# A two-layer graph kernel on one core: eight places lent once, the first 128 chunks of `src` and x loaded first, the rest of `src` and `dst` turned later

## The chip, the core and the metric

The kernel runs on one core of one Trainium2 chip. The metric is the device time of one execution in microseconds. The core has five instruction streams that matter here: TensorE (PE) for matrix products, VectorE (DVE), ScalarE (ACT), GpSimd (POOL), which issues the indirect DMAs (gathers of rows by a list of indices), and SyncE (SP), which issues the plain DMAs. Each stream runs in its written order and waits on semaphores for the others.

## The reference

x has 6250 rows of 512 floats; `src` and `dst` are the two ends of 100,000 edges, sorted by `dst`.

```python
h = jnp.maximum(_layernorm(x, axis=-1), 0.0)
norm = -dinv[src] * dinv[dst]                 # dinv = 1/sqrt(number of edges that leave a node), or 0
def _cheb_conv(x, src, dst, norm, W0, W1, b):
    out = x @ W0
    tx1 = segment_sum(x[src] * norm[:, None], dst, num_segments=N)
    return out + tx1 @ W1 + b
h = _cheb_conv(h, src, dst, norm, W1_0, W1_1, b1)
h = _layer_norm(h, gamma, beta)
h = jnp.where(h >= 0, h, 0.01 * h)
out = _cheb_conv(h, src, dst, norm, W2_0, W2_1, b2)
return x + out
```

## The kernel before

**Chunks and steps.** The sorted edges are cut into NC = 782 chunks of 128. For each layer, one gather on GpSimd fetches the 128 source rows of a chunk (256 KB) into a *place* in SBUF. A 128x32 matrix `sel` of zeros and ones then adds them up by target node: `ps[32 rows] += sel.T @ rows`. Three chunks make a unit with its own 32 rows of `ps`, four units make a step, so a step sums 12 chunks (L630, in `sums`), in the order s = 0, 1, 2 and within it q = 0 to 3. There are NS = 66 steps (`g` in `usual_path`); step 0 has one unit and chunks 0 to 2, step g has chunks 12g - 9 to 12g + 2, and the last step has 11. The sums of a step are copied to `agg` (L641), and `place` (L661) distributes them over blocks of 128 nodes with a second matrix, `there`. For each of the 49 node blocks there are then the transposes (L526 for the block's own rows `h`, L769 for the summed rows `an`) and the products with the two weight matrices (L538), a layer norm in layer one, and the stores.

**Places.** A gather needs a free place. There are X = 12 lent ones at first (the two weight tiles `w`, 4 places each, and the four bias tiles, which are loaded with their own contents later) and those of the tile `places`, with 63 rows of 528 floats. The last 8 of its rows are kept for the second layer's weights (`w_late`), so R = 55 are left, and chunk k uses row `(k - X) % R`. Chunk k can be gathered once chunk k - 55 has been summed. The first RAW = 76 chunks are gathered from x itself, before the table of normalised rows is complete, and are normalised in their place afterwards (`find`, `look_up`, L483 to L509). Later chunks come from the table `tab`, whose 16 extra columns carry `dinv`.

**The setup** (up to about 108 us). SP loads `src_i`, the chunk form of `src` and `dst`, and x, block by block, into rows 14 to 62 of `places`. `src` has to be turned, so that a chunk lies along the partitions: cast by VectorE, transposed by TensorE (L233), copied to `sidx` by ScalarE (L235); only then can GpSimd issue its first gather (L239). `dst` is turned likewise into `dlx` (L257 to L261). VectorE counts the edges of each source node: 25 groups, in each of which two comparisons make matrices `lo` and `hi` (L343) that TensorE multiplies (L357). ScalarE meanwhile computes means and variances of the x blocks (`stats`) and normalises them (`make_table`, L314); SP writes a pair of blocks to `tab`, and the two places of that pair can then take a gather (`gather_raw`). `turns` says at which counting group which x blocks are taken.

**The order of the work.** In the setup, only SP's order is the written one and the other engines' is set by a scheduler from the dependences; `issue_after` keeps an instruction behind another. In the main part, TensorE, GpSimd and SP follow the program's order (`manual_schedule`). There, a step first issues the gathers that are allowed (`gather_to`), then works off the blocks that are complete (`finished`, which calls `turn` with the transposes of `h` and `place`), then makes `sel` and takes its sums. In the steps of `SOON` = 4 and 5 of layer one, the sums come ahead of `finished`.

**The end of a layer.** In step 64 and 65 the sums are cut into pieces with the work of the last blocks between them; `place_end` (L684), `end_block` (L692) and `end_products` treat the last block, with 106 rows.

Of the kernel before, what the change touches and what calls it, by code (L numbers as in the profile page):

```python
# [20 lines left out]
P = 128  # L21
# [22 lines left out]
def gnn_kernel(  # L44
# [111 lines left out]
    for lo, hi in parts(EP):  # L156
        nc.sync.dma_start(src_i[lo:hi], src[lo * EJ : hi * EJ].rearrange("(p j) -> p j", j=EJ))


    nc.gpsimd.memset(eps, EPS)  # L160
    nc.gpsimd.memset(places[:, :, D:], 1.0)
    nc.scalar.activation(root_eps, eps, AF.Sqrt)
    FG = NC // P - (E % (P * P) == 0)
    chunks = []
    for ids, fill, name in ((src, 0, "src_c"), (dst, NO_NODE, "dst_c")):
        t = ep.tile([P, NG, P], I32, name=name)
        nc.gpsimd.memset(t[:, FG:, :], fill)
        nc.sync.dma_start(t[:, :FG, :], ids[: FG * P * P].rearrange("(g c e) -> c g e", c=P, e=P))
# [7 lines left out]
        chunks.append(t)  # L176


# [15 lines left out]
    nc.gpsimd.memset(places[:, RE + NB - 1, :D], 0.0)  # L194
    for i0, n in groups[:6]:
        load_x(i0, n)

    def load_rest(k):
# [6 lines left out]
        if k == 4:  # L205
            for t, v in ((bias1, b1), (bias2, b2), (gam, gamma), (bet, beta)):
# [7 lines left out]
    nc.gpsimd.iota(diff, pattern=[[1, P]], base=0, channel_multiplier=-1,  # L214
                   allow_small_or_imprecise_dtypes=True)
# [6 lines left out]
    nc.gpsimd.memset(ones, 1.0)  # L222


    nc.vector.tensor_single_scalar(ident, diff, 0.0, op=OP.is_equal)
    with tc.tile_pool(name="turn", bufs=1) as wp, tc.tile_pool(
        name="turn_ps", bufs=2, space=bass.MemoryType.PSUM
    ) as wps:
        f = wp.tile([P, NG, P], F32, name="f")
        nc.vector.tensor_copy(f, chunks[0])  # L230
        for g in range(NG):
            fT = wps.tile([P, P], F32, name="fT")
            nc.tensor.transpose(fT, f[:, g, :], ident)  # L233
            n = min(P, NC - g * P)
            nc.scalar.activation(sidx[:, g * P : g * P + n], fT[:, :n], AF.Copy)  # L235

    def gather_raw(lo, hi):
        for t in range(lo, min(hi, X + R)):
# [5 lines left out]

    low = ep.tile([P, P], I32, name="low")
    nc.vector.tensor_single_scalar(low, chunks[0][:, 0, :], P - 1, op=OP.bitwise_and)
    nc.vector.tensor_copy(src_lo, low)
    nc.vector.tensor_copy(pick, ident)


    nc.vector.memset(dlx[:, 0:1], 0.0)
    nc.vector.memset(dlx[:, 1 + NC :], float(N))
    with tc.tile_pool(name="turn", bufs=1) as wp, tc.tile_pool(
        name="turn_ps", bufs=1, space=bass.MemoryType.PSUM
    ) as wps:
        f = wp.tile([P, NG, P], F32, name="f")
        nc.vector.tensor_scalar_add(f, chunks[1], 1.0)  # L257
        dl_ps = wps.tile([P, NG * P], F32, name="dl_ps")
        for g in range(NG):
            nc.tensor.transpose(dl_ps[:, g * P : (g + 1) * P], f[:, g, :], ident)  # L260
        nc.scalar.activation(dlx[:, 1 : 1 + NC], dl_ps[:, :NC], AF.Copy)  # L261
        last = ident[:, P - 1 : P]
        first_ps = nodes_ps[:, : NQ * NS + 1]
        nc.tensor.matmul(first_ps, last.to_broadcast([P, P]), dlx[:, 0 : STEP * NQ * NS + 1 : STEP], start=True, stop=True)
        nc.vector.tensor_copy(first, first_ps)
        row_ps = wps.tile([P, NS], F32, name="row_ps")
        for q in range(NQ):
            for g, n in ((0, 1), (1, NS - 1)):
# [54 lines left out]
    for k in range(2):  # L323
        stats(*some[k])

    both = ep.tile([P, NB, 2, 2], F32, name="both")
    with tc.tile_pool(name="deg", bufs=1) as dp, tc.tile_pool(name="onehot", bufs=2) as ohp, tc.tile_pool(
# [11 lines left out]
        for g in range(EJ // (2 * GJ)):  # L339
# [9 lines left out]
            if k is not None:  # L349
# [4 lines left out]
                if k + 2 < len(some):  # L354
                    stats(*some[k + 2])
# [53 lines left out]
def usual_path(tc, have):  # L409
# [19 lines left out]
    with ExitStack() as es:  # L429
# [175 lines left out]
        def scale(sel, chunk, of=(0, NQ)):  # L605
# [4 lines left out]
            if end <= RAW:  # L610
                return
# [704 lines left out]
```

## Time and profile before

| | us |
|---|---|
| median of 3 runs | 2026.56 (2023.77 to 2027.43) |
| profiled execution | 2031.79 |
| span in that profile | 2030.0 |
| TensorE busy | 1662.7 (82%) |
| GpSimd busy | 1522.9 (75%) |
| VectorE busy | 708.7 (35%) |
| ScalarE busy | 414.0 (20%) |
| first gather issued at | 8.14 |
| last gather issued at | 2009.57 |

The profile is of one execution. A line of a timeline gives start, duration, engine, source line, operation, output and input, the number of instructions merged, and in brackets the idle time of the engine ahead of it with what ended that. A line of groups gives busy time and mean duration, then the idle time ahead and what ended most of it; "issue" there means that the engine waited for nothing that the profile shows. For a row by stage the columns are the stretch, its length, busy time by engine with the number of instructions, the granted TensorE clock, the share of time that the DMA engines were busy, and GB/s. A DMA instruction on GpSimd is busy while it is issued; its data land later.

### The profile page before, as it was taken

How to read it: one execution, taken by the hardware profiler on the slowest of the kernel's cores; microseconds unless marked ns; L12 is line 12 of the kernel's file. 1: busy time of each engine (PE TensorE's matmuls, PEld its weight loads, DVE VectorE, ACT ScalarE, POOL GpSimd, SP SyncE). 2: the span in 40 equal slices, each digit the busy share in tenths (PEclk: the TensorE clock that was granted, in tenths of full speed). 3: DMA queues.
4: the chain of work that ended last, by engine and by line, in shares of the span. 5: the costliest groups of instructions: out<-in, count | busy, mean ns of one | idle time of the engine just before them, and what ended most of it. 6: DMA issues, size and time to landing. Idle time of an engine off the chain costs nothing.

```text
span 2030.0 us, 20088 instructions
## 1 busy us (share of the span) xinstructions
PE 1662.7 (82%) x6907; PEld 667.6 (33%) x6907; DVE 708.7 (35%) x1494; ACT 414.0 (20%) x750; POOL 1522.9 (75%) x1578
## 2 busy tenths in 40 slices
PE   4579998777887776878879888888888888888987
PEld 3544443223333222333323322323322332333333
DVE  7965543332453333443453111122211212222211
ACT  8795221111221111221211100101010101011100
POOL 7867777777777777777777777777777777777774
PEclk9779998889898889989998998999998999999999
DMA  9998888888888888888887888888887888788875
GB/s 343 374 355 247 268 277 254 253 244 261 282 276 261 248 254 250 267 254 267 242 259 239 257 251 251 243 255 248 245 257 246 245 253 256 240 262 252 272 236 165
DMA packets 190115, 528.40 MB, mean 260 GB/s; under 512 B 34637, under 2 KB 36411, under 8 KB 190005
## 3 DMA queue, kind: packets, MB, share of 16 engines
q0 software_dynamic: 125120, 415.88, 68.4%
q1 hardware_dynamic: 64844, 111.14, 15.2%
q8 instruction: 56, 0.92, 0.2%
q14 instruction: 55, 0.44, 0.1%
q10 hardware_dynamic: 40, 0.02, 0.0%
HBM read 475.25 MB, written 51.66 MB: 260 GB/s over the span
## 4 chain that ended last, share of the span: by engine, by line
PE 45%; DMA 25%; POOL 12%; issue 10%; DVE 6%; ACT 1%; POOLq 0%; DVEq 0%; SPq 0%; ACTq 0%
DMA places<-tab,sidx 19%; PE u_ps L538 18%; PE ps L630 14%; POOL places L450 12%; PE an_ps L661 8%; DMA places<-tab,lidx 5%; PE hT_ps L526 2%; PE hT_ps L769 2%; DVE hi L343 1%; DVE lo L343 1%; PE hT_ps L498 1%; DMA h<-tab 1%; DVE sel L617 0%; DVE st L729 0%; DMA tab<-places 0%
## 5 line engine op out<-in xcount | busy, mean ns | idle before, releaser
L450 POOL DMA_INDIRECT places<-tab,sidx x1191 | 1130.6, 949 | 368.0 <-issue 262.6
L630 PE MATMUL ps<-places,sel 128*32 128x512 f32 x3104 | 505.1, 660 | 149.9 <-DMA places<-tab,sidx 84.9
L661 PE MATMUL an_ps<-agg,there 128*128 128x512 f32 (+1 forms) x554 | 273.7, 627 | 96.2 <-ACT agg L641 90.9
L450 POOL DMA_INDIRECT places<-tab,lidx x270 | 255.4, 946 | 82.2 <-issue 62.4
L630 PEld LDWEIGHTS ps<-places,sel 128*32 128x32 f32 x3104 | 100.7, 116 | 520.6 <-issue 182.8
L577 DVE TENSOR_TENSOR sel<-dlx,nodes_ps 128x384 f32<-128x384 f32 (+3 forms) x134 | 72.3, 541 | 409.8 <-PE ps L630 409.8
L538 PE MATMUL u_ps<-w,hT 128*128 128x512 f32 (+1 forms) x400 | 184.9, 606 | 21.2 <-ACT hT L528 20.5
L641 ACT ACTIVATE agg<-ps 128x512 f32<-128x512 f32 (+1 forms) x128 | 76.0, 593 | 565.2 <-PE ps L630 539.2
L538 PE MATMUL u_ps<-places,hT 128*128 128x512 f32 (+2 forms) x408 | 183.2, 593 | 3.2 <-ACT hT L528 3.2
L661 PEld LDWEIGHTS an_ps<-agg,there 128*128 128x128 f32 (+1 forms) x554 | 106.6, 201 | 219.6 <-issue 110.7
L538 PE MATMUL u_ps<-w,aT 128*128 128x512 f32 x384 | 173.4, 594 | 2.6 <-DVE aT L771 2.5
L538 PE MATMUL u_ps<-places,aT 128*128 128x512 f32 x384 | 173.4, 593 | 0.8 <-DVE aT L771 0.8
L617 DVE TENSOR_TENSOR sel<-sel,places 128x384 f32<-128x384 f32 (+11 forms) x71 | 34.3, 488 | 339.2 <-DMA places<-tab,sidx 328.6
L720 DVE TENSOR_TENSOR u_ps<-u_ps,bias 128x512 f32<-128x512 f32 x45 | 31.5, 700 | 282.5 <-PE u_ps L538 282.5
L528 ACT ACTIVATE hT<-hT_ps 128x512 f32<-128x512 f32 (+1 forms) x98 | 58.2, 594 | 279.7 <-PE hT_ps L526 278.9
L649 DVE TENSOR_SCALAR there<-iota_r,node_of 128x128 f32<-128x128 f32 (+1 forms) x286 | 86.2, 304 | 70.6 <-PE an_ps L661 68.0
L762 ACT ACTIVATE an<-an_ps,ndinv 128x512 f32<-128x512 f32 x96 | 65.8, 685 | 216.4 <-PE an_ps L661 216.4
L538 PEld LDWEIGHTS u_ps<-w,hT 128*128 128x128 f32 (+1 forms) x400 | 73.5, 194 | 97.0 <-issue 74.7
L732 ACT ACTIVATE sd<-mv,eps 128x1 f32<-128x1 f32 (+1 forms) x49 | 14.4, 294 | 437.8 <-DVE mv L730 431.1
L538 PEld LDWEIGHTS u_ps<-places,hT 128*128 128x128 f32 (+1 forms) x408 | 74.7, 193 | 77.5 <-issue 72.1
L538 PEld LDWEIGHTS u_ps<-w,aT 128*128 128x128 f32 x384 | 70.4, 190 | 83.4 <-issue 76.9
L538 PEld LDWEIGHTS u_ps<-places,aT 128*128 128x128 f32 x384 | 70.6, 190 | 80.3 <-issue 78.3
(193 smaller groups left out, 1341.1 us busy)
## 6 DMA issues: line engine op xcount, KB each, us to landing
places<-tab,sidx POOLq DMA_INDIRECT x1191, 4.0
h_tab<-g SPq DMA_DIRECT2D x48, 256.0 KB
xt<-in_x_dram SPq DMA_DIRECT2D x48, 256.0 KB
out_dram<-t SPq DMA_DIRECT2D x48, 256.0 KB
tab<-t SPq DMA_DIRECT2D x46, 256.0 KB
tab<-places SPq DMA_DIRECT2D x22, 528.0 KB
h<-tab SPq DMA_DIRECT2D x45, 256.0 KB
h<-h_tab SPq DMA_DIRECT2D x45, 256.0 KB
```

What stands on the lines that cost most here:

```text
L343: nc.vector.tensor_tensor(t, s[:, g * 2 * GJ : (g + 1) * 2 * GJ].rearrange("p (j s) -> p j s", s=2)[:, :, None, :] .to_broadcast([EP, GJ, ...
L450: nc.gpsimd.indirect_dma_start(out=places[:, (t - X) % R, :] if own_scale else zr(layer, t), out_offset=None, in_=x if layer == 0 and t < ...
L526: nc.tensor.transpose(ps[:, kc, :r], h[:r, kc * P : (kc + 1) * P], ident[:r, :r])
L528: nc.scalar.activation(hT[:, :, :r], ps[:, :, :r], AF.Copy)
L538: nc.tensor.matmul(u_ps[:r], hT[:, kc, :r], w[:, kc, :], start=(start and kc == 0), stop=(stop and kc == KD - 1))
L577: nc.vector.tensor_tensor(sel[:, q : q + k, :w, :], of, node[:, q : q + k, None, :].to_broadcast([P, k, w, Q]), op=OP.is_equal)
L630: nc.tensor.matmul(ps[q * Q : (q + 1) * Q, :], sel[:, q, s, :], zr(layer, chunk[q][s]), start=(s == 0), stop=(s == len(chunk[q]) - 1 and ( ...
L641: nc.scalar.activation(agg[g][: n * Q], ps[: n * Q], AF.Copy)
L649: behind[1] = nc.vector.tensor_scalar(t[:m, :r], iota_r[:m, :r], node_of[:m, g : g + 1], -(1.0 + i * P), op0=OP.subtract, op1=OP.is_equal)
L661: nc.tensor.matmul(placed[i][:r], t[:m, :r], agg[g][:m, :], start=(g == inside[i][0]), stop=(g == inside[i][-1]))
L762: nc.scalar.activation(an[:r], placed.pop(i)[:r], AF.Copy, scale=ndinv[:r, i : i + 1])
L769: nc.tensor.transpose(ps[:, kc, :r], an[:r, kc * P : (kc + 1) * P], ident[:r, :r])
```

## The change

Five things are changed.

1. *The order of loading.* SP issues the first 128 chunks of `src` (one 128x128 piece) first, then the first x blocks, and the rest of `src`, `dst` and `src_i` between further x blocks. Two fills of `places` on GpSimd go behind its iotas; `ident` is made first.
2. *Turning in pieces.* Only the first 128x128 piece is cast, transposed and copied to `sidx` ahead of the first gather. The other pieces of `src` are turned in counting group 1 and `dst` in group 2, each cast in its own tile.
3. *Eight places lent.* The last eight rows of `places` are used once, for chunks 67 to 74 (`gather_raw` goes up to `X + RE + NB` = 75); `slot` gives the row of a chunk, and in layer one `gather_to` allows eight chunks more up to chunk 129. From chunk 130 on it is again 55 chunks.
4. *`SOON`* is 3 to 5 instead of 4 and 5.
5. *The ends.* In layer two, step 64 takes its sums for the first two units of the step, then for the other two. The last `agg` copy and the copy of `end_block` are cut into halves.

The program order of SP at the start, before:

```order
1 L157 DMA src_i<-in_src_dram 112x800
2 L157 DMA src_i<-in_src_dram 13x800
3 L168 DMA src_c<-in_src_dram 128x6x128
4 L171 DMA src_c<-in_src_dram 13x128
5 L174 DMA src_c<-in_src_dram 1x32
6 L168 DMA dst_c<-in_dst_dram 128x6x128
7 L171 DMA dst_c<-in_dst_dram 13x128
8 L174 DMA dst_c<-in_dst_dram 1x32
9 L188 DMA places<-in_x_dram 128x2x512
10 L188 DMA places<-in_x_dram 128x4x512 x3
11 L188 DMA places<-in_x_dram 128x7x512 x2
```

And the same place on SP now:

```order
1 L160 DMA src_c<-in_src_dram 128x128
2 L186 DMA places<-in_x_dram 128x2x512
3 L196 DMA src_i<-in_src_dram 112x800
4 L196 DMA src_i<-in_src_dram 13x800
5 L186 DMA places<-in_x_dram 128x4x512
6 L160 DMA src_c<-in_src_dram 128x5x128
7 L165 DMA src_c<-in_src_dram 13x128
8 L168 DMA src_c<-in_src_dram 1x32
9 L186 DMA places<-in_x_dram 128x4x512
10 L160 DMA dst_c<-in_dst_dram 128x6x128
11 L165 DMA dst_c<-in_dst_dram 13x128
12 L168 DMA dst_c<-in_dst_dram 1x32
```

One 128x128 piece of `src` and two x blocks have moved to the front; `dst` has moved behind ten x blocks.

TensorE at step 3 of layer one, before:

```order
949 L483 MATMUL hT_ps<-src_lo,pick 128x128
950 L526 MATMUL hT_ps<-ident,h 128x128 x4
951 L661 MATMUL an_ps<-agg,there 128x512
952 L661 MATMUL an_ps<-pre,there 128x512
953 L661 MATMUL an_ps<-agg,there 128x512
954 L630 MATMUL ps<-places,sel 32x512 x12
955 L498 MATMUL hT_ps<-sc,xt 128x98 x4
```

And now:

```order
954 L510 MATMUL hT_ps<-src_lo,pick 128x128
955 L657 MATMUL ps<-places,sel 32x512 x12
956 L553 MATMUL hT_ps<-ident,h 128x128 x4
957 L690 MATMUL an_ps<-agg,there 128x512
958 L690 MATMUL an_ps<-pre,there 128x512
959 L690 MATMUL an_ps<-agg,there 128x512
960 L525 MATMUL hT_ps<-sc,xt 128x98 x4
```

The twelve sums of step 3 stand ahead of the transposes of `h` and of the first placement.

TensorE in the last steps of layer two, before:

```order
1793 L661 MATMUL an_ps<-agg,there 128x512 x3
1794 L630 MATMUL ps<-places,sel 32x512 x4
1795 L769 MATMUL hT_ps<-ident,an 128x128 x4
1796 L630 MATMUL ps<-places,sel 32x512 x4
1797 L538 MATMUL u_ps<-places,aT 128x512 x4
1798 L630 MATMUL ps<-places,sel 32x512 x4
1799 L661 MATMUL an_ps<-agg,there 128x512 x2
1800 L630 MATMUL ps<-places,sel 32x512 x5
```

And now:

```order
1798 L690 MATMUL an_ps<-agg,there 128x512 x3
1799 L657 MATMUL ps<-places,sel 32x512 x4
1800 L800 MATMUL hT_ps<-ident,an 128x128 x4
1801 L657 MATMUL ps<-places,sel 32x512 x2
1802 L565 MATMUL u_ps<-places,aT 128x512 x4
1803 L657 MATMUL ps<-places,sel 32x512 x6
1804 L690 MATMUL an_ps<-agg,there 128x512 x2
1805 L657 MATMUL ps<-places,sel 32x512 x5
```

The twelve sums of step 64 are cut into 4, 2 and 6 instead of 4, 4 and 4, and the first six are those of two units.

The diff, cut to its core:

```diff
+    load_chunks(chunks[0], src, 0, 1)
+    nc.gpsimd.iota(diff, pattern=[[1, P]], base=0, channel_multiplier=-1,
+                   allow_small_or_imprecise_dtypes=True)
+    made = nc.vector.tensor_single_scalar(ident, diff, 0.0, op=OP.is_equal)
...
+    load_x(*groups[0])
+    for lo, hi in parts(EP):
+        nc.sync.dma_start(src_i[lo:hi], src[lo * EJ : hi * EJ].rearrange("(p j) -> p j", j=EJ))
+    load_x(*groups[1])
+    load_chunks(chunks[0], src, 1, FG)
+    load_end(chunks[0], src)
+    load_x(*groups[2])
+    load_chunks(chunks[1], dst, 0, FG)
+    load_end(chunks[1], dst)
+    for i0, n in groups[3:6]:
         load_x(i0, n)
...
+    def turn_src(wps, to, lo, hi):
+        copied = nc.vector.tensor_copy(to, chunks[0][:, lo:hi])
+        for g in range(lo, hi):
+            fT = wps.tile([P, P], F32, name="fT")
+            nc.tensor.transpose(fT, to[:, g - lo, :], ident)
+            n = min(P, NC - g * P)
+            turned = nc.scalar.activation(sidx[:, g * P : g * P + n], fT[:, :n], AF.Copy)
+        return copied, turned
...
     def gather_raw(lo, hi):
-        for t in range(lo, min(hi, X + R)):
+        for t in range(lo, min(hi, X + RE + NB)):
...
+            if g in (1, 2):
+                with tc.tile_pool(name="turn_ps", bufs=3 - g, space=bass.MemoryType.PSUM) as wps:
+                    (turn_rest, turn_dst)[g - 1](wps)
...
-    SOON = range(4, 6)
+    SOON = range(3, 6)
...
+        LATER = places.shape[1] - R
+        def slot(k):
+            return k - X if k < X + R + LATER else (k - X - LATER) % R
...
+            end = summed_to + R
+            if layer == 0:
+                end = max(end, min(end + LATER, X + LATER + 2 * R))
...
+                w = D // 2 if g == NS - 1 else D
+                for lo in range(0, D, w):
+                    nc.scalar.activation(agg[g][: n * Q, lo : lo + w], ps[: n * Q, lo : lo + w], AF.Copy)
...
+            for lo in range(0, KD, KD // 2):
+                nc.vector.tensor_copy(aT[:, lo : lo + KD // 2, :r], ps[:, lo : lo + KD // 2, :r])
...
-                    step = [[(s, q) for q in range(NQ)] for s in range(STEP)]
+                    if layer:
+                        half = [[(s, q) for s in range(STEP) for q in range(at, at + NQ // 2)] for at in (0, NQ // 2)]
+                        step = [half[0][:-2], half[0][-2:], half[1]]
+                    else:
+                        step = [[(s, q) for q in range(NQ)] for s in range(STEP)]
```

More of the change, by code (lines that the diff above doesn't have):

```diff
@@ L322, in gnn_kernel @@
     turns = {1: 0, 4: 1, 7: 2, 11: 3, 17: 4, 21: 5}
-    for k in range(2):
-        stats(*some[k])
+    with tc.issue_after(turned.ins):
+        for k in range(2):
+            stats(*some[k])
     both = ep.tile([P, NB, 2, 2], F32, name="both")
```

141 lines of the change are left out of this document (66 added, 75 removed).

## The prediction, before the result was known

> **What bounds the kernel now.** I read the page first, then GpSimd's groups and its busy time by stage, then its timeline at every place where it idled longer than usual, then TensorE and the end. In the page, POOL is not the busiest engine; the row of its groups says why it still bounds.
>
> ```profile
> PE 1662.7 (82%) x6907; PEld 667.6 (33%) x6907; DVE 708.7 (35%) x1494; ACT 414.0 (20%) x750; POOL 1522.9 (75%) x1578
> ...
> L450 POOL DMA_INDIRECT places<-tab,sidx x1191 | 1130.6, 949 | 368.0 <-issue 262.6 <-DMA places<-tab,sidx 52.4 <-PE ps L630 26.5
> ...
> 0.00:8.14 8.14, 3.66 (x14) 1.00 0.75 212
> 8.14:92.19 84.05, 71.86 (x41) 0.90 1.02 375
> 92.19:128.60 36.41, 27.57 (x30) 0.72 1.03 366
> 128.60:152.02 23.42, 12.44 (x13) 0.78 1.05 331
> 152.02:2010.52 1858.50, 1407.34 (x1482) 0.93 0.83 254
> 2010.52:2030.00 19.48, 0.00 (x1) 0.97 0.18 60
> ```
>
> The columns of the last six rows are: stretch, its length, POOL's busy time and instructions, granted TensorE clock, DMA share, GB/s. From 152.02 to 2010.52 there are 1482 gathers in 1858.50 us, one per 1.254 us (0.949 busy and 0.30 of issue), with nothing else between them. GpSimd issues without a pause for 92% of the span, so the end is: when GpSimd leaves 152, plus a fixed number of gathers, plus the 19.48 us behind the last one. Only four things can be shortened: the 8.14 us ahead of the first gather, the slow stretch to 92.19, the hole before 152.02, and the tail.
>
> The slow stretch: 40 gathers (the 41st begins at its border) in 84.05 us, where 40 x 1.254 = 50.2 would do, so 33.9 us are lost. The timelines of VectorE and GpSimd say to whom.
>
> ```profile
> 28.71 1.78 DVE L343 TENSOR_TENSOR hi<-s_hi,iota_g 125x3136 bf16<-125x3136 bf16 x1
> 30.41 1.22 DVE L343 TENSOR_TENSOR lo<-s_lo,iota_g 125x2048 bf16<-125x2048 bf16 x1
> 31.55 1.78 DVE L343 TENSOR_TENSOR hi<-s_hi,iota_g 125x3136 bf16<-125x3136 bf16 x1
> ...
> 28.78 2.53 POOL L239 DMA_INDIRECT places<-in_x_dram,sidx  x1 [0.30 <-issue]
> 31.62 2.53 POOL L239 DMA_INDIRECT places<-in_x_dram,sidx  x1 [0.30 <-issue]
> ...
> 92.19 0.95 POOL L239 DMA_INDIRECT places<-in_x_dram,sidx  x1 [0.30 <-issue]
> ```
>
> A gather that begins 0.07 us behind a `hi` takes 2.53 us instead of 0.95, and ends about 0.9 us after that `hi` does; then the next one begins just behind the next `hi`. GpSimd falls into step with the 2.84 us of a counting group and issues one gather per group. The last `hi` is over before 92.19, and from there each takes 0.95, though the DMA share stays 1.03. So I put the loss down to VectorE's 25 counting groups, not to the DMA engines: 33.9 / 25 = 1.36 us a group, 1.59 (2.84 - 1.25) where it is locked. [...]
>
> **The change, part by part.** *Earlier first gather.* The chain of before:
>
> ```profile
> 0.74 0.89 SPq L157 DMA_DIRECT2D src_i<-in_src_dram  x2
> 2.68 0.25 SPq L174 DMA_DIRECT2D src_c<-in_src_dram  x1
> ...
> 5.85 0.23 DVE L246 TENSOR_SCALAR low<-src_c 128x128 int32<-128x128 int32 x1 [4.94 <-DMA src_c<-in_src_dram]
> 6.25 0.62 DVE L230 CAST f<-src_c 128x896 f32<-128x896 int32 x1
> 7.07 0.69 PE L233 MATMUL fT<-ident,f 128*128 128x128 f32 x2 [7.07 <-DVE p_i L274]
> 7.58 0.49 ACT L235 ACTIVATE sidx<-fT 128x128 int32<-128x128 f32 x2 [5.34 <-PE fT L233]
> 8.14 1.10 POOL L239 DMA_INDIRECT w<-in_x_dram,sidx  x1 [3.91 <-ACT sidx L235]
> ```
>
> Now the 128x128 piece of `src` is SP's first DMA instead of its third to fifth; SP issued its first at 0.74. From the end of the last issue to VectorE's read were 5.85 - 2.93 = 2.92 us; 0.74 + 0.40 + 2.92 = 4.06 is the late end for the new landing, and 3.0 the early one (a smaller DMA, nothing ahead of it). Behind it: a 128x128 copy as `low`, 0.23; transpose 7.07 to 7.58, 0.51; ScalarE to GpSimd 0.56; 1.3 together. The first gather is issued between 4.3 and 5.4; GpSimd's own start-up (3.66 us busy from 0.74 on, the same instructions reordered) ends at 4.2 either way. I take 4.9, a gain of 3.2 (2.7 to 3.8). It is kept only if the counting costs the same 33.9 us, and it is the same 25 groups; locked in all of them it would be 39.8, which is 5.9 worse, and I allow as much the other way.
>
> *Counting earlier, rest turned later.* `src_i` keeps its place near the front (third), VectorE no longer does the seven-column casts and `dst` first, and the first x block no longer stands behind eight other DMAs, so ScalarE starts its sums some 4 us before the 10.68 of before:
>
> ```profile
> 10.68 0.63 ACT L294 ACTIVATE junk<-places 128x512 bf16<-128x512 f32 x1 [1.98 <-DMA places<-in_x_dram]
> ...
> 16.54:91.07 74.53, 45.29 (x399) 39.70 (x399) 73.66 (x68) 65.24 (x154) 64.47 (x34) 0.89 1.02 375
> ```
>
> In this row (PE, PEld, DVE, ACT, POOL busy) VectorE is full from 16.54 to 91.07 and ScalarE 88%, so both follow an earlier start. Against it: the turned pieces now sit inside groups 1 to 5, where TensorE's counting matmuls queue behind transposes of `dst`, and these behind ScalarE's copy `dlx`, which is its 29th row. I estimate ScalarE there at about 28 us, and VectorE at its wait at about 27. Counting should end 3.5 us earlier (1 to 5). This is worth nothing by itself, since GpSimd bounds; it is the cover for the next part. `dst` landing later, the moved fills and iotas and the in-place casts add nothing: no gather waits for them.
>
> *Eight places lent, and block sums ahead of the first placement.* GpSimd's only long holes:
>
> ```profile
> 131.35 1.10 POOL L450 DMA_INDIRECT places<-in_x_dram,sidx  x1 [1.80 <-PE ps L630]
> 133.08 0.94 POOL L450 DMA_INDIRECT places<-in_x_dram,sidx  x1 [0.64 <-ACT places L509]
> ...
> 152.02 0.94 POOL L450 DMA_INDIRECT places<-tab,sidx  x1 [5.49 <-PE ps L630]
> ...
> 142.63 1.09 PE L526 MATMUL hT_ps<-ident,h 128*128 128x128 f32 x4 [3.74 <-DMA h<-tab]
> 143.64 2.07 PE L661 MATMUL an_ps<-agg,there 32*128 32x512 f32 x2
> 149.36 3.74 PE L630 MATMUL ps<-places,sel 128*32 128x512 f32 x24
> 206.66 2.78 PE L630 MATMUL ps<-places,sel 128*32 128x512 f32 x24
> 219.84 2.35 PE L630 MATMUL ps<-places,sel 128*32 128x512 f32 x20
> ```
>
> Beyond the usual 0.30 these are 1.50 + 0.34 + 5.19 = 7.03 us. The gather at 152.02 is chunk 82; it needs the place of chunk 27, summed in step 3 at 149.36. With eight more places, chunk 82 needs chunk 19, summed long before, and up to chunk 129 GpSimd may be eight chunks, 10 us, further ahead. Besides, step 3's sums now stand ahead of the transposes that waited 3.74 us for `h`, so they run in that hole at about 140. All three waits go. What is late next is chunk 130, where the lead shrinks to 55: it needs chunk 75, step 7, summed at 206.66. GpSimd issued chunk 130 at 152.02 + 48 x 1.254 = 212.2; now at 212.2 - 7.0 - 3.2 = 202.0. TensorE must be 206.66 - 202.0 = 4.7 us earlier there. It gets 3.7 from the filled hole and 3.5 from the earlier counting: 7.2, which is 2.5 to spare. Step 8 (219.84 against 227.2 - 10.2 = 217.0) needs only 2.8. I take the full 7.0.
>
> Chunk 76 is the first from the table, and waits for all writes of it, the small ones of `dinv` too. It comes at 134 instead of 139.33; the queue that carries those writes held SP's next issue until 131.19:
>
> ```profile
> 123.23 7.96 SPq L204 DMA_DIRECT2D w<-in_L_gnn_W_dram  x1
> ```
>
> I price a wait there at 0 to 3 us and take 0, since the counting ahead of them is earlier as well.
>
> *The tail.*
>
> ```profile
> 1993.32 5.06 DMA places<-tab,lidx
> ...
> 1998.43 1.92 PE L630 MATMUL ps<-places,sel 128*32 128x512 f32 x2 [2.79 <-DMA places<-tab,lidx]
> 2006.94 1.99 PE L661 MATMUL an_ps<-agg,there 128*128 128x512 f32 x4
> 2008.86 2.76 PE L630 MATMUL ps<-places,sel 128*32 128x512 f32 x10
> 2014.91 2.77 PE L630 MATMUL ps<-places,sel 128*32 128x512 f32 x12
> 2009.57 0.95 POOL L450 DMA_INDIRECT places<-tab,lidx  x1 [0.30 <-issue]
> DMA to landing us min/median/max: 3.5/3.9/7.2
> ```
>
> The step before the last took its sums in rounds over all four quarters and so waited 2.79 us for the tenth of its twelve chunks; from 2000.28 on TensorE is busy until 2018.7, so the wait moves the end. Now it takes two quarters first. Two quarters at a time cost 2.77 / 6 = 0.46 us a sum (the x12 row is such an order; 24 passes over four quarters also take 2.78). From 1994.58: four sums 1.85, transposes 0.66, two sums 0.92, products 3.70, six sums 2.77: at the placement by 2004.5 instead of 2006.94, 2.4 us earlier, all the way to the last sums (2012.5 instead of 2014.91). The last gather lands 3.9 us after 2009.57, 2013.5, in time for the sum that needs it. Halving the two last copies gives at most 0.3, since products of the block before run beside them. I take 2.6; a landing of 7.2 leaves 0, and the whole wait and copies are 3.1.
>
> **Sum:** 3.2 + 7.0 + 2.6 = 12.8 us. The profiled execution took 2031.79 (span 2030.0), so 2019.0 of it remain. It stands 5.23 above the median of the runs, 2026.56; taken off that, 2013.8.
>
> **Rivals.** *One: the early start is lost in the DMA.* The stretch 8.14 to 92.19 has a DMA share of 1.02 at 375 GB/s; if that sets its pace, starting sooner only lets gathers displace the same loads, and 2013.8 + 3.2 = 2017.0. For it: the share; against it: the pace jumps at 92.19 while the share stays. [...]
>
> *Two: the wait moves to chunk 130.* If counting is no earlier and the filled hole gives nothing, TensorE reaches step 7 at 206.66 and GpSimd waits 4.7 of the 12.8 back: 2018.5.
>
> *Three, slower: the turned `dst` holds up the counting.* If `dlx` comes so late that counting, and with it step 7, ends D later than before, GpSimd waits at chunk 130 for 4.7 + D - 3.7. This exceeds 12.8 from D = 11.8 on; at D = 18, 2033. ScalarE would have to reach `dlx` near 45 us. Its 65.24 us of 74.53 speak for a queue there; its earlier start speaks against.
>
> *Four: nothing that can be told* (0.2%, 4 us, is about what a measurement of this kernel can tell): counting locks GpSimd in every group (5.9 back) and rival two holds (4.7): 2024.4.
>
> **Chances.** Forecast 0.52, one 0.17, two 0.14, four 0.09, three 0.08. Below 2022.5 lie the first three: faster 0.83; the fourth is the same, 0.09; slower 0.08. The range goes from 2006.5 (counting costs 5.9 less, and the better ends) to 2022.5, past rivals one and two.
>
> **What would show it.** The first gather near 4.9; 0.95 us gathers at once behind the last `hi`, near 88; no gap over 0.6 at chunks 70, 82 and 130; step 3's sums before the transposes of `h`; no wait of 2.79 in the last steps, and about 16.9 us from the last gather to the end. It is wrong if the counting stretch loses more than 40 us, or a wait for `ps` opens near 200.

## The result, and the profile after

The changed kernel took 2019.72 us (median of 10 runs, 2017.84 to 2024.82) beside 2024.26 of the kernel before (10 runs on the same chip): ratio 0.9975, 95% interval 0.9966 to 0.9984, so 5 us faster (3 to 7). On a second chip it was 0.9956 (0.9940 to 0.9972). The forecast was 2013.8, a gain of 12.8; the sign and the range held, the size didn't. The time looks closer than the gain by chance: the kernel before itself came out 2.3 us faster here (2024.26) than the 2026.56 from which the forecast started. The profiled executions took 2031.79 before and 2024.52 after, 7.3 us apart.

The page of the changed kernel, its busy times and GpSimd's largest group:

```profile
PE 1667.6 (82%) x6907; PEld 666.7 (33%) x6907; DVE 709.5 (35%) x1497; ACT 413.8 (20%) x752; POOL 1523.8 (75%) x1578
...
L477 POOL DMA_INDIRECT places<-tab,sidx x1191 | 1129.1, 948 | 362.8 <-issue 250.4
```

No engine has more than 5 us more or less to do. By stage (stretch, length, busy time of PE, PEld, DVE, ACT, POOL with instructions, granted clock, DMA share, GB/s):

```profile
5.44:93.38 87.94, 51.17 (x447) 43.42 (x447) 86.61 (x121) 76.56 (x183) 75.45 (x41) 0.87 1.02 376
93.38:152.00 58.62, 45.35 (x292) 27.32 (x296) 42.06 (x101) 51.27 (x75) 44.61 (x47) 0.87 1.04 371
152.00:2000.87 1848.87, 1554.83 (x6108) 588.18 (x6101) 575.83 (x1270) 282.79 (x489) 1399.23 (x1476) 0.92 0.82 255
2000.87:2022.60 21.73, 15.78 (x68) 7.55 (x66) 2.90 (x6) 1.35 (x3) 0.94 (x1) 0.94 0.20 66
```

The third row again has one gather per 1.25 us without a hole. Chunk k's gather is the k-th, counted from 0. The first row ends at chunk 41: it was issued at 93.38, and at 93.44 before. So the 2.7 us by which the first gather came earlier (5.44 instead of 8.14) were gone by then. The second row holds 47 gathers in 58.62 us, 1.25 each: there the three waits are gone. The last gather is issued at 2000.87, 8.7 us earlier than 2009.57, but from there to the end it takes 21.7 us instead of 20.4. Of the 8.7 us, 7.2 are there at chunk 82 (144.85, was 152.02). The other 1.5 came along the gathers behind it, and that is within chance: from chunk 90 to the last gather it took 1846.0 to 1852.5 us in twelve executions of these kernels.

The setup, first VectorE and GpSimd at the start, then three of GpSimd's gathers beside the counting and the first one behind it:

```profile
2.61 1.70 DVE L236 CAST f<-src_c 128x128 f32<-128x128 int32 x1 [1.13 <-DMA src_c<-in_src_dram]
5.44 1.10 POOL L250 DMA_INDIRECT w<-in_x_dram,sidx  x1 [1.22 <-ACT sidx L241]
8.41 1.21 DVE L359 TENSOR_TENSOR lo<-s_lo,iota_g 125x2048 bf16<-125x2048 bf16 x1
...
48.33 9.98 POOL L250 DMA_INDIRECT places<-in_x_dram,sidx  x1 [0.30 <-issue]
58.62 0.94 POOL L250 DMA_INDIRECT places<-in_x_dram,sidx  x1 [0.30 <-DMA tab<-places]
81.79 2.53 POOL L250 DMA_INDIRECT places<-in_x_dram,sidx  x1 [0.30 <-issue]
84.63 0.95 POOL L250 DMA_INDIRECT places<-in_x_dram,sidx  x1 [0.30 <-issue]
```

The first piece of `src` landed sooner than forecast (the cast begins at 2.61), but that cast took 1.70 us. Counting began 8 us earlier than before (8.41, was 16.54) and ended at 83.5 instead of 91.07. One gather hung for 9.98 us across three counting groups; the longest of the kernel before was 4.30. This one and chunk 41, both before:

```profile
55.76 4.30 POOL L239 DMA_INDIRECT places<-in_x_dram,sidx  x1 [0.30 <-issue]
93.44 0.95 POOL L239 DMA_INDIRECT places<-in_x_dram,sidx  x1 [0.30 <-ACT places L314]
```

The place of the former holes, on GpSimd and TensorE:

```profile
136.04 0.95 POOL L477 DMA_INDIRECT places<-in_x_dram,sidx  x1 [0.30 <-issue]
137.29 1.00 POOL L477 DMA_INDIRECT places<-tab,sidx  x1 [0.30 <-issue]
144.85 0.95 POOL L477 DMA_INDIRECT places<-tab,sidx  x1 [0.30 <-issue]
...
132.49 2.76 PE L657 MATMUL ps<-places,sel 128*32 128x512 f32 x18 [0.32 <-ACT places L536]
135.48 0.63 PE L553 MATMUL hT_ps<-ident,h 128*128 128x128 f32 x4 [0.23 <-DMA h<-tab]
195.46 2.78 PE L657 MATMUL ps<-places,sel 128*32 128x512 f32 x24
```

Chunk 82 goes out at 144.85 (152.02 before) with no wait, step 3's sums stand at 132.49 ahead of the transposes of `h`, and step 7, which frees the place of chunk 130, is summed at 195.46 (206.66 before).

The end. First a row of the chain of work, the gather for whose landing TensorE waited:

```profile
1972.14 6.25 DMA places<-tab,lidx
```

then rows of TensorE's timeline (transposes and some products left out), step 63 up to 1981.48 and step 64 from 1989.91:

```profile
1978.43 1.22 PE L657 MATMUL ps<-places,sel 128*32 128x512 f32 x2 [2.18 <-DMA places<-tab,lidx]
1981.48 5.93 PE L565 MATMUL u_ps<-places,aT 128*128 128x512 f32 x8 [0.78 <-DVE aT L802]
1987.25 2.74 PE L690 MATMUL an_ps<-agg,there 128*128 128x512 f32 x6
1989.91 1.91 PE L657 MATMUL ps<-places,sel 128*32 128x512 f32 x8
1992.35 1.05 PE L657 MATMUL ps<-places,sel 128*32 128x512 f32 x4
1996.96 2.77 PE L657 MATMUL ps<-places,sel 128*32 128x512 f32 x12
1999.66 1.98 PE L690 MATMUL an_ps<-agg,there 128*128 128x512 f32 x4
```

and three stages, with columns as above (the granted clock stands third from the end):

```profile
1970.00:1980.00 10.00, 7.46 (x33) 2.09 (x33) 2.16 (x5) 0.94 (x2) 7.57 (x9) 0.96 0.79 236
1980.00:1985.00 5.00, 4.22 (x8) 1.81 (x7) 0.69 (x1) 0.35 (x1) 3.79 (x5) 0.50 0.73 213
1985.00:1990.00 5.00, 5.00 (x13) 1.99 (x13) 1.30 (x3) 0.00 (x0) 3.78 (x5) 0.90 0.73 204
```

Two rows of the same place before, the products of step 63 and the placement behind them:

```profile
1988.38 3.70 PE L538 MATMUL u_ps<-places,aT 128*128 128x512 f32 x8 [0.78 <-DVE aT L771]
1991.91 2.74 PE L661 MATMUL an_ps<-agg,there 128*128 128x512 f32 x6
```

Step 64's wait is gone: from the placement at 1987.25 to the one at 1999.66 are 12.41 us, 15.03 before (1991.91 to 2006.94). But one step earlier TensorE now waited 2.18 us for a landing, the granted clock then fell to 0.50, and eight products took 5.93 us, which had taken 3.70 before. The placement at 1987.25 stands 13.6 us ahead of the last gather; before it stood 17.7 ahead.

### The profile page after: what moved, and what is told of

It is laid out like the page before. It is cut to its first block, busy times and chain, and to the rows that moved or that the text cites. A ratio compares the mean times of both kernels' runs of the same rounds, so it can differ in the third digit from the quotient of the medians.

```text
span 2022.6 us, 20097 instructions
## 1 busy us (share of the span) xinstructions
PE 1667.6 (82%) x6907; PEld 666.7 (33%) x6907; DVE 709.5 (35%) x1497; ACT 413.8 (20%) x752; POOL 1523.8 (75%) x1578
## 4 chain that ended last, share of the span: by engine, by line
PE 46%; DMA 29%; POOL 10%; issue 8%; DVE 5%; ACT 2%; POOLq 0%; DVEq 0%; ACTq 0%
DMA places<-tab,sidx 20%; PE u_ps L565 20%; PE ps L657 13%; POOL places L477 10%; PE an_ps L690 9%; DMA places<-tab,lidx 6%; PE hT_ps L800 2%; PE hT_ps L553 2%; DVE hi L359 1%; DVE lo L359 1%; DMA w<-in_L_gnn_W_dram 1%; DMA tab<-places 0%; DVE st L760 0%; DVE sel L644 0%; DMA src_c<-in_src_dram 0%
## 5 line engine op out<-in xcount | busy, mean ns | idle before, releaser
L657 PE MATMUL ps<-places,sel 128*32 128x512 f32 x3104 | 516.1, 669 | 145.5 <-DMA places<-tab,sidx 79.2
L690 PE MATMUL an_ps<-agg,there 128*128 128x512 f32 (+1 forms) x554 | 270.3, 621 | 96.4 <-ACT agg L670 91.3
L565 PE MATMUL u_ps<-w,hT 128*128 128x512 f32 (+1 forms) x400 | 186.2, 609 | 21.7 <-ACT hT L555 20.9
L670 ACT ACTIVATE agg<-ps 128x512 f32<-128x512 f32 (+2 forms) x130 | 76.1, 587 | 569.2 <-PE ps L657 543.2
L250 POOL DMA_INDIRECT places<-in_x_dram,sidx x63 | 89.5, 1421 | 19.2 <-issue 9.4
## 6 DMA issues: line engine op xcount, KB each, us to landing
tab<-places SPq DMA_DIRECT2D x22, 528.0 KB, 10.2
```

Of the source, the lines that this page charges most:

```text
L250: nc.gpsimd.indirect_dma_start(out=lent[t] if t < X else places[:, t - X, :D], out_offset=None, in_=x, in_offset=bass.IndirectOffsetOnAxis ...
L565: nc.tensor.matmul(u_ps[:r], hT[:, kc, :r], w[:, kc, :], start=(start and kc == 0), stop=(stop and kc == KD - 1))
L657: nc.tensor.matmul(ps[q * Q : (q + 1) * Q, :], sel[:, q, s, :], zr(layer, chunk[q][s]), start=(s == 0), stop=(s == len(chunk[q]) - 1 and ( ...
L670: nc.scalar.activation(agg[g][: n * Q, lo : lo + w], ps[: n * Q, lo : lo + w], AF.Copy)
L690: nc.tensor.matmul(placed[i][:r], t[:m, :r], agg[g][:m, :], start=(g == inside[i][0]), stop=(g == inside[i][-1]))
```

## Experiments

**Theory**: of the three terms the lent places are real, the early start is taken back by the counting groups, and the ends are worth less than one execution's wait. **Rivals**: the three add up as forecast; the order of loading or the new ends do harm; the DMA sets the pace of the setup.

### Each part alone, and in pairs

e1 has the lent places and `SOON` = 3 to 5 alone, on the kernel before (with `slot` and `gather_to` as in the change); e3 the ends alone; e2 the loading and turning alone, made from the changed kernel:

```diff
-            for t in range(lo, min(hi, X + RE + NB)):
+            for t in range(lo, min(hi, X + R)):
...
-    SOON = range(3, 6)
+    SOON = range(4, 6)
...
-        LATER = places.shape[1] - R
+        LATER = 0
...
```

The last part, left out here, puts the ends back as they were before.

> The kernel before with only the eight lent places and SOON = 3 to 5; loading, turning and the ends as before. Theory (the three waits of 1.50, 0.34 and 5.19 us at chunks 70, 71 and 82 go and nothing takes their place): 7.0 us under the kernel before, and the first 42 gathers lose 34 us as before. Rival (the wait moves to chunk 130, or the other parts of the change were needed to keep step 7 early enough): a gap of 1 to 5 us near 205 us on GpSimd, and 2 to 5 us in all.

> The changed kernel without the lent places, with SOON = 4 and 5, and with the ends as before: only the order of loading and the turning in pieces. Theory A (while VectorE counts, GpSimd goes at the pace of the counting groups, so gathers begun earlier only spend longer locked): first gather at 5.4 instead of 8.1, gather 41 at 93.4 as in both, time within 1 us of the kernel before. Theory B (the 9.98 us gather of the changed kernel was an accident of that execution): 2.7 us faster, gather 41 near 90.7. Theory C (the turned dst holds something up): slower by 1 us or more.

> The kernel before with only the order of step 64 in layer two and the two halved copies. Theory T1 (the order saves the wait for the tenth chunk; in the profile of the changed kernel a late landing and a lower granted clock hid it): 2.6 us faster, and about 16.9 us from the last gather's end to the end. Theory T2 (TensorE is the bound behind about 1979 us, so the wait that goes is only a pause that it had anyway): 0 to 0.5 us, and 19 to 20 us behind the last gather.

Ratios to the kernel before: e1 0.9975 (0.9965 to 0.9985), e2 0.9982 (0.9971 to 0.9993), e3 0.9985 (0.9976 to 0.9994). All three help. In e1 no wait opened at chunk 130, so its rival falls; the gain of 5.1 us (3.0 to 7.1) just contains the 7.0 of its theory. In e2 theory C falls, and theory A too: it allowed 1 us and gather 41 at 93.4, and e2 was 3.7 us faster (1.4 to 5.9) with gather 41 at 91.20, which fits theory B (2.7 us, 90.7). In e3 the gain is 3.0 us (1.2 to 4.9), and from the last gather's end to the end it took 16.5 us, as theory T1 said (16.9). Then the whole and the pairs:

> The changed kernel once more, beside the pairs of its parts. The parts alone gave 0.25% (lending), 0.18% (loading) and 0.15% (ends) under the kernel before, 11.8 us together. Theory S (the parts add up, and the 5.0 us of the whole were few runs): ratio 0.9942, about 11.8 us faster. Theory M (they don't add: what loading gains at the front is taken back by the blocks of the table that come no earlier, or by a counting stretch that costs more): ratio 0.9975 as measured, 5 us.

> Lent places, SOON = 3 to 5 and the ends, with loading and turning as before. S: 8.1 us under the kernel before. M with loading as the spoiler: 7 to 8 us, and faster than the whole change by 2 to 3 us.

> The changed kernel with the ends as before. S: 8.8 us under the kernel before. M with loading as the spoiler: 4 to 5 us, no better than lending alone. If instead the new ends are the spoiler when GpSimd is early: 8 to 9 us, and faster than the whole change.

> The changed kernel without the lent places and with SOON = 4 and 5. S: 6.7 us under the kernel before. M: 3 to 4 us, and the wait at chunk 82 (6.87 us with loading alone, 5.19 before) stays.

e5 (whole) 0.9956 (0.9940 to 0.9972), e6 0.9980 (0.9967 to 0.9993), e7 0.9973 (0.9963 to 0.9983), e8 0.9982 (0.9971 to 0.9993). The pairs gained 4.1, 5.5 and 3.7 us. Theory S's 8.1, 8.8 and 6.7 lie above the interval of each, while its 11.8 for the whole lies inside (5.7 to 12.2); but S adds up single measurements with errors of their own. A least-squares fit to all 148 times on these three chips (one level per chip, one term per part) gives lending 3.4, loading 2.25, ends 1.2 us, each with a standard error of 0.5: 6.8 together. Terms for the pairs were 1.1, 1.5 and -0.2, each with an error of 1.1, so neither that the parts add up exactly nor that they don't is shown. No part is a spoiler.

The traces of these runs show the three terms one by one. *Waits between chunks 66 and 90, beyond 1.25 us a gather*: without lent places 7.2, 7.0, 6.1 and 5.9 us (before, e2, e3, e8); with them 0.2, 0.0, 0.2 and 0.2 (changed, e5, e6, e7). In e1 2.0 were left, in one place:

```profile
134.13 0.95 POOL L458 DMA_INDIRECT places<-in_x_dram,sidx  x1 [0.30 <-issue]
137.26 0.95 POOL L458 DMA_INDIRECT places<-tab,sidx  x1 [2.18 <-DMA tab<-dinv]
...
113.22 1.42 SPq L396 DMA_DIRECT2D tab<-dinv  x1
```

This is chunk 76, the first from the table, waiting for the small write of `dinv`, issued at 113.22. In the changed kernel that write is issued 6.5 us earlier:

```profile
106.69 1.54 SPq L415 DMA_DIRECT2D tab<-dinv  x1
```

There chunk 76 did not wait. Nor did it in e6, which has the old loading and issued that write at 113.29: there chunk 41 had come at 95.17 (91.34 in e1), and GpSimd reached chunk 76 only at 139.12. So the wait is one of single executions, in which GpSimd is early and the write late.

### What sets the pace while VectorE counts

e4 is the changed kernel with every second pair of comparisons left out; e10 does this too and compares with numbers in PSUM. Both thus count the edges wrongly.

```diff
-            hot = []
-            for s, n, name in ((s_lo, LO, "lo"), (s_hi, HI, "hi")):
+            if g % 2 == 0:
+                hot = []
+            for s, n, name in ((s_lo, LO, "lo"), (s_hi, HI, "hi")) if g % 2 == 0 else ():
...
+        iota_ps = dps.tile([P, HI, 2], F32, name="iota_ps")
+        nc.vector.tensor_copy(iota_ps, iota_g)
...
-                    iota_g[:EP, None, :n, :].to_broadcast([EP, GJ, n, 2]), op=OP.is_equal)
+                    iota_ps[:EP, None, :n, :].to_broadcast([EP, GJ, n, 2]), op=OP.is_equal)
```

> The changed kernel in which every second counting group takes the two matrices of the group ahead of it, so that VectorE makes 13 pairs instead of 25 (the edge counts, and all that follows from them, are then wrong; every other instruction stays). Lock theory: the first 42 gathers lose about 19 us instead of 36.7, and gathers of 0.95 us stand in the stretches where VectorE makes none; the time falls by up to 17 us, less what GpSimd then waits for blocks of the table. DMA theory (the 1.02 share sets the pace): the gathers' mean in that stretch and the 36.7 us stay within 3 us, and so does the time.

> As the kernel with half of the counting groups (edge counts wrong), and the comparisons read the numbers they compare with from PSUM, in 4-byte form, instead of from SBUF; 13 pairs. If VectorE's second input from SBUF is what locks GpSimd out, every gather beside a comparison takes 0.95 us, though VectorE is busier than with half of the groups; what then ends GpSimd's waits are blocks of the table. If VectorE locks it out in any case, or the DMA does, gathers of 1.4 to 2.5 us stay, and the first 30 gathers lose more than 8 us in their own length.

In e4 the first 41 gathers exceeded 0.95 us by 11.4 us in their own length, instead of 36.5 in the changed kernel, at the same DMA share of 1.02. In e10, a single execution on the first of two chips described below, they exceeded 0.95 us by 0.4 us in sum. The longest, 1.29 us, began before the first comparison; 27 of the first 42 gathers stood beside a comparison, and none of these took more than 1.02:

```profile
37.12 3.42 DVE L362 TENSOR_TENSOR hi<-s_hi,iota_ps 125x3136 bf16<-125x3136 bf16 x1
...
36.02 0.94 POOL L250 DMA_INDIRECT places<-in_x_dram,sidx  x1 [0.30 <-issue]
37.26 0.94 POOL L250 DMA_INDIRECT places<-in_x_dram,sidx  x1 [0.30 <-issue]
46.10 0.94 POOL L250 DMA_INDIRECT places<-in_x_dram,sidx  x1 [7.89 <-ACT junk L270]
```

In e10 a gather begun 0.14 us behind a `hi` took 0.94 us, with the second operand in PSUM. In the changed kernel, with both operands in SBUF, 12 of the first 41 gathers took 2.52 to 2.56, one 4.30 and one 9.98 us. So the lock was gone in this execution, where VectorE's second input no longer came from SBUF. (That operand also went from 2 to 4 bytes, and the comparison got slower, 3.42 us instead of 1.78; these were not taken apart.)

But the freed gathers bought no time. e4's ratio was 0.9970 (0.9957 to 0.9983), like the changed kernel's, and its GpSimd now waited for other things:

```profile
56.64 0.95 POOL L250 DMA_INDIRECT places<-in_x_dram,sidx  x1 [6.17 <-ACT junk L266]
86.97 0.94 POOL L250 DMA_INDIRECT places<-in_x_dram,sidx  x1 [6.75 <-DMA tab<-places]
140.15 0.94 POOL L478 DMA_INDIRECT places<-tab,sidx  x1 [4.07 <-DMA tab<-dinv]
```

Its stage up to chunk 41:

```profile
5.44:88.22 82.78, 43.90 (x447) 40.05 (x447) 57.24 (x99) 64.64 (x164) 50.27 (x41) 0.85 1.02 375
```

Chunk 41 came at 88.22, 5.2 us earlier than in the changed kernel, and chunk 76 at 140.15, 2.9 us later. The DMA moved 375 GB/s here and 376 in the changed kernel. The x blocks and the writes of the table, all of which chunk 76 needs, came later: an x load was issued at 64.77 instead of 58.82, the write of `dinv` at 116.72 instead of 106.69. This fits rival one's mechanism as a second wall behind the lock, but it does not show it. In e4 the scheduler had put a piece of work on an x block ahead of VectorE's last two pairs of comparisons (in the changed kernel it stands behind the last one); VectorE waited 13.24 us there for that block, up to 62.90, and ScalarE then 12.07 us for VectorE. How much of the new waits is the DMA's pace and how much this order stays open.

### The early start by itself

e9, e13 and e18 are one kernel, the changed one with one line moved:

```diff
-    load_chunks(chunks[0], src, 0, 1)
...
     load_x(*groups[1])
+    load_chunks(chunks[0], src, 0, 1)
     load_chunks(chunks[0], src, 1, FG)
```

> The changed kernel with the first piece of src loaded behind the first two groups of x and src_i instead of ahead of all (one line moved), so that the first gather comes some 3 us later, near 8.5 us; all else as changed. Theory A (the pace of the counting groups and the lot of each gather in them decide when gather 41 is issued, so the early start is worth at most 1 us): within 1 us of the changed kernel, gather 41 at 91 to 95 as in its five executions so far. Theory B (the early start is worth what the first gather shows): 3 us slower than the changed kernel.

> The changed kernel with the first piece of src loaded behind the first two groups of x and src_i, so that the first gather is issued about 10.2 us (as on the chip of e9) instead of 5.4. Theory A (the counting groups set GpSimd's pace and take the early start back): within 1 us of the changed kernel, gather 41 at 91 to 95. Theory B: 3 to 5 us slower than the changed kernel.

> The changed kernel with its first gather at 10.2 us instead of 5.4. Theory A (the counting groups take the early start back; in e9 and e13 gather 41 came at 91.8 and 91.9, with the early start at 90.7 to 94.7): 6 to 7 us under the kernel before, as the changed kernel. Theory B (the start is worth what the first gather shows): 2 us under it.

Here is chunk 0 and chunk 41 of e13:

```profile
10.17 1.10 POOL L250 DMA_INDIRECT w<-in_x_dram,sidx  x1 [5.94 <-ACT sidx L241]
...
91.88 0.94 POOL L250 DMA_INDIRECT places<-in_x_dram,sidx  x1 [0.30 <-issue]
```

| setup, executions | first gather | chunk 41 (mean) | lost to chunk 41, beyond 41 x 1.25 |
|---|---|---|---|
| before: before, e1, e3, e6, e16 | 8.1 to 8.5 | 91.3 to 96.3 (93.7) | 32.0 to 36.8 |
| changed: ten executions | 5.4 (4.5 once) | 90.6 to 94.7 (92.5) | 33.9 to 38.0 |
| late start: e9, e13, e18 | 10.2 to 10.7 | 91.8, 91.9, 96.1 (93.2) | 30.4 to 34.1 |

A first gather 5 us later moves chunk 41 by 0.7 us; one 2.7 us earlier by 1.2, where single executions of one setup differ by 4 to 5, so that each of these two means has an error of 1 to 1.5 us. e18's ratio was 0.9975 (0.9962 to 0.9988), 5.1 us under the kernel before with 2.4 to 7.7: theory A's 6 to 7 lies in it, theory B's 2 just outside. So the late start costs clearly less than the 5 us that the first gather shows. What the early one is worth is not settled this closely: the whole of the new loading gave 2.25 us in time by the fit, of which chunk 41 shows 1.2.

e9 and e13 ran on two chips on which the kernel before took 2451 and 2462 us, and their ratios were within their errors of 1 (e9 0.9991, e13 1.0003); behind chunk 74 the engines of those executions paused for microseconds for nothing that the profile shows (VectorE once for 14.86 us in e9), so only stretches without such pauses are used. For the same reason the two bases said nothing (e12 1.0001, e15 0.9993), though their chunk 41 (91.83 and 92.84) is in the table.

> The changed kernel once more, as the base for the two kernels ahead of it on the same chip: 6.8 us under the kernel before by the sum of the parts fitted over all runs so far (lending 3.4, loading 2.2, ends 1.2), with the first 42 gathers losing 34 to 38 us.

> The changed kernel, as the base for the others on this chip: 5 to 8 us under the kernel before (5.0 and 8.9 measured so far, 6.8 from the sum of the parts fitted over all runs).

### What bounds the end

From the placement of step 63 to the end of the span, worked out from TensorE's timelines, with the wait inside step 64 in brackets: the order of before 38.1 (2.79; before), 36.4 (2.44; e2), 35.8 (0.93; e1), 33.5 (none; e7). The order of the change 35.3 to 35.8 in six executions (changed, e3, e5, e6, e8, e18) and 36.7 in e4, whose end came 1.2 us later behind TensorE's last product; none has a wait in step 64. The rows of e7, the old order without a wait:

```profile
1994.03 2.74 PE L688 MATMUL an_ps<-agg,there 128*128 128x512 f32 x6
1996.70 1.07 PE L657 MATMUL ps<-places,sel 128*32 128x512 f32 x8
1998.28 1.24 PE L657 MATMUL ps<-places,sel 128*32 128x512 f32 x8
2003.08 1.06 PE L657 MATMUL ps<-places,sel 128*32 128x512 f32 x8
```

The twelve sums take 1.07 + 1.24 + 1.06 = 3.4 us side by side over four quarters, and 1.91 + 1.05 + 2.77 = 5.7 two by two. From the placement of step 63 to the next one the new order took 12.4 us in all seven executions; the old one took 15.0 with the wait of 2.79 and 10.0 in e7. So the new order saves 2.6 us where the wait is 2.79, and loses 2.4 where there is none. Another order uses three quarters at first and needs the tenth chunk later (e11, e14 and e17 are the changed kernel with it, e16 the lent places with it and no new loading):

```diff
-                        half = [[(s, q) for s in range(STEP) for q in range(at, at + NQ // 2)] for at in (0, NQ // 2)]
-                        step = [half[0][:-2], half[0][-2:], half[1]]
+                        z = NQ - 1
+                        step = [[(0, q) for q in range(z)], [(1, q) for q in range(z)] + [(0, z)],
+                                [(1, z)] + [(2, q) for q in range(NQ)]]
```

> The changed kernel with another order in step 64 of layer two: the first sums of three quarters, then their second sums with the first one of the last quarter, then the rest, so that three or four quarters go side by side (5.73 us of sums in the changed kernel, about 4.1 here), and the tenth chunk is needed about 1.3 us later than before. If TensorE bounds the end in the changed kernel (35.5 us from the placement of step 63 to the end in all five executions with the new order), 1.3 to 1.6 us faster than the changed kernel, and about 34 us in that stretch. If GpSimd's last gathers bound it, no difference.

> The changed kernel with step 64 of layer two in the order by three quarters. If TensorE bounds the end: 1.3 to 1.6 us faster than the changed kernel, and 34.2 us (as on the chip of e11) from the placement of step 63 to the end, against 35.5. If the last landings bound it: no difference.

> Lent places, SOON = 3 to 5, and the ends with step 64 by three quarters; loading and turning as before the change. If loading adds nothing to the lent places: as e14, 7 to 9 us under the kernel before. If loading is worth its 2.2 us there too: 2 us slower than e14.

> The changed kernel with step 64 of layer two in the order by three quarters. If TensorE bounds the end: 8.2 us under the kernel before (the changed kernel is 6.8 under it by the fit over all its runs on the first three chips, and 1.4 us go), and about 34 us from the placement of step 63 to the end. If the last landings bound it: 6.8.

The stretch took 34.2, 33.9 and 33.7 us in e11, e14 and e16, beside 35.3 to 35.4 in the change's order on the same chips (e9, e12, e13, e15). There the last gather had been issued over 20 us before the stretch, and TensorE's rows show no wait for a landing in it: its work is 1.4 us shorter, as expected. In e17 it took 36.6, with the wait back:

```profile
1983.23 2.74 PE L690 MATMUL an_ps<-agg,there 128*128 128x512 f32 x6
1987.47 1.06 PE L657 MATMUL ps<-places,sel 128*32 128x512 f32 x6
1990.09 1.05 PE L657 MATMUL ps<-places,sel 128*32 128x512 f32 x2 [1.56 <-DMA places<-tab,lidx]
```

In time e17 had 0.9962 (0.9948 to 0.9977), which contains both 6.8 and 8.2 us: no better than the changed kernel that can be told. e11 (0.9969, 0.9941 to 0.9998), e14 (0.9998) and e16 (1.0000) ran on the two chips above. So neither side of the question holds alone: TensorE's work bounds the end when it is behind, a landing when it has caught up. How far it is behind shows in the same placement: it stood 13.6, 14.0 and 15.0 us ahead of the last gather in the three executions whose clock fell to 0.50 in step 63 (changed, e5, e7), and 16.6 to 18.5 in the other nine on chips without pauses, whose clock stayed at 1.00 there.

## Why the prediction was right or wrong

**Bound and sign: right.** GpSimd's gathers bound the kernel before and after, 1476 of them in 1848.87 us, and the time lies in the range given. Rival two's 2018.5 came nearest to the measured 2019.72, by chance: its wait at chunk 130 isn't there.

**The sum in the profiled pair.** The spans differ by 7.4 us where 12.8 had been forecast: the start kept 0.1 of its 3.2, the lent places gave their 7.1, the main part 1.5, within its scatter, and the end lost 1.3 where it should have gained 2.6.

**Earlier first gather (3.2): the first gather right, its worth wrong.** 5.44 was just past the late end of the bounds (4.3 to 5.4). The step that failed is "it is kept only if the counting costs the same 33.9 us, and it is the same 25 groups": I took the loss for a fixed toll. It is no toll of so many groups: while VectorE counts, whether a gather enters in this group or the next but two differs from execution to execution (one gather of 4.30, 7.6 or 9.98 us decides), and the loss ran from 32.0 to 36.8 in one and the same setup. The changed kernel's profile lost 36.7, which ate the 2.7 whole; over all executions about 1.2 was left at chunk 41, with an error of 1. The bound of 39.8 that I had worked out was the honest warning, and I gave it no weight in the sum. Rival one priced this loss with the wrong mechanism in front: it was the lock that set the gathers' pace (beyond 0.95 us each they lost 36.5 us in the changed kernel, 11.4 in e4 and 0.4 in e10), and the DMA may be a wall behind it (e4, not shown).

**Counting earlier, rest turned later: right in sign, too small.** Counting ended 7.6 us earlier instead of 3.5; the turned `dst` held nothing up, so rival three fell, and rival two too: chunk 130 found its place free.

**Lent places (7.0): right on GpSimd, less in time.** The waits that went are 6.4 us over the executions (6.5 to 0.15). In time lending alone gave 5.1 (3.0 to 7.1), and the fit over all runs 3.4, the largest shortfall of the three. The step that failed is "I take the full 7.0": it puts what GpSimd no longer waits down as time, one for one. Where the rest goes is open. In the nine profiled executions of the two kernels, the parts and the pairs, the last gather is issued 5.4 us earlier in the mean with the lent places, and from there to the end it takes 1.3 us longer (19.6 and 18.4), where single executions differ by 4.5. So some of it may be lost at TensorE's end, which isn't shown. The wait for `dinv` that I priced at 0 to 3 us and took as 0 was 1.88 in e1, and 0 in the changed kernel.

**The tail (2.6): right for the one execution, wrong as a term.** From placement to placement I had forecast 2.4, and it was 2.6 (15.03 to 12.41). But the wait of 2.79 was the longest of four (2.79, 2.44, 0.93, 0), and the new order costs 2.4 when there is none; the fit gives 1.2 for all of the ends. I had also written that the last gather fixes the end by "about 16.9 us". In e3, e6 and e8 it was 16.3 to 16.5, with the clock at 1.00 in step 63. In the changed kernel it was 20.8, with something in front that I hadn't foreseen: a wait of 2.18 us in step 63 was followed by the clock at 0.50 from 1979.2 to 1986.0, and behind that TensorE was 4 us further behind GpSimd than before (its placement stood 13.6 instead of 17.7 us ahead of the last gather).

**The signs.** Right: no gap at chunks 70, 82 and 130, step 3 ahead of the transposes, 0.95 us gathers at once behind the last `hi`, no 2.79 in step 64. Wrong: 20.8 us from the last gather's end to the end, not 16.9. By the fit the terms came to 2.25 + 3.4 + 1.2 = 6.8 where I had 3.2 + 7.0 + 2.6: each had been taken at what one profiled execution showed.

## What to carry to other kernels

Before a gain is booked from a single profile, ask which of its waits would be as long in the next execution: here what the lock took varied by 4.8 us in one setup (32.0 to 36.8), the wait for a landing in step 64 by 2.8 (0 to 2.79), and eight products took 5.93 or 3.70 with and without a clock drop; that is as much as the terms themselves. Ask of an earlier start whether it is still there behind the next stretch: here 2.7 us at the first gather were about 1.2 behind the counting. A reordering that avoids a wait by doing work less in parallel has a price when the wait isn't there (here 2.6 us saved with the wait of 2.79, 2.4 lost with none), and both belong in the sum.

## What the runs showed of the hardware that I had not expected

Beside VectorE's comparisons with both operands in SBUF, a gather's issue took up to 9.98 us, over three groups, in the changed kernel, though of the 14 that took over 2.5 us there 12 stayed at 2.52 to 2.56; in e10, with the second operand in PSUM, none took more than 1.02 beside a comparison.

TensorE's granted clock was 0.50 behind several of its waits of 1.8 to 2.8 us. In the kernel before, the wait of 2.00 us up to 1963.23 was followed by 0.50 from 1963.82 on, which pulls down the clock of this row, and during the one of 2.79 up to 1998.43 it fell to 0.50 again, at 1997.95; in the changed kernel 2.18 us was followed by 0.50 from 1979.2 to 1986.0, in e5 1.79 by 0.50 from 1981 on.

```profile
1960.00:1970.00 10.00, 5.39 (x20) 1.00 (x21) 0.00 (x0) 0.00 (x0) 7.56 (x9) 0.69 0.75 210
```

It didn't always follow: 2.44 us up to 1996.97 in e2 and 1.88 up to 1979.25 in e1 left the clock at 1.00. What decides it is not shown. Where it followed, a wait of TensorE near the end came twice: in the changed kernel 2.18 us as a wait, then eight products of 5.93 us instead of 3.70.
